# Unread TensorE products behind the last products of each Sobel layer and among the last small products of the layer norm

## The chip, the cores and the metric

The kernel runs on one core of one Trainium2 chip. The metric is the time of one execution on the device in microseconds (us). The kernel before took 2829.04 us, the median of three runs (2828.97 to 2829.38).

## What is computed

The input is an image of 256 x 256 positions with 32 channels in float32. Four layers follow, and each adds its output to its input after a group norm (16 groups). Cut to what matters:

```python
# layer 0: a layer norm over channels, then gated values (the softmax runs over an axis of length 1)
mn = (m - mu) * rsqrt(var + 1e-5) * ln_gamma + ln_beta
x = x + (sigmoid(mn @ Wg) * (mn @ Wv)) @ Wo + bo
# layers 1 and 2: Sobel magnitude of a 3-wide average along one axis
pooled = avg_pool3_same(v)               # v = group_norm(x)
x = x + sqrt(gx(pooled)**2 + gy(pooled)**2 + 1e-6)
# layer 3: two LSTM-like cells with a group norm of the gates, 256 steps in sequence
for t in range(256):
    z = x_t @ W_lat + b_lat
    for j in range(2):
        zz = group_norm([z, h[j]] @ W_cell[j] + b_cell[j])   # 4 groups of 128
        i, f, o, g = split(zz)
        c[j] = sigmoid(f) * c[j] + sigmoid(i) * tanh(g)
        h[j] = sigmoid(o) * tanh(c[j]); z = z + h[j]
    out_t = x_t + z @ W_out + b_out
```

## The kernel before, in words

The image stays in SBUF as `xa` and `xb`: 128 partitions hold four neighbouring columns times 32 channels, and 64 blocks of 256 positions lie along the free axis. Two blocks together, a tile of 128 x 512, are called a pair; there are 32 pairs. The stages run one after the other.

**Input** (to about 42 us). The image is loaded, transposed on TensorE and copied, and statistics for the first group norm are taken.

**Layer norm.** A first loop makes centred values of each pair, squares them on ScalarE and sums the squares with small products into `pvar` (line 247). Then `std`, a `table` load for the sigmoid and `reciprocal` give `rstd` (lines 267 to 269); nine unread products of 128 x 256 run meanwhile (line 271). Then comes the second loop, over the 32 pairs. A product of 32 rows (line 278, `spread` times `rstd`, 128 x 512) spreads the reciprocal deviations over all partitions into a PSUM tile `pb`; VectorE multiplies the pair by it (line 285); ScalarE and GpSimd in turn apply gamma and beta (lines 287 and 291). Four pairs after each other use the four groups of 32 rows in turn. The pool `ps_sp` has eight buffers, one PSUM bank each, so TensorE can be eight products ahead of VectorE. Behind the loop stand four unread products of 128 x 256 (line 296), in one more tile of that name.

**Attention.** The order is written out by hand. Products of 32 rows make values `pv` and gates `pg` (line 313), ScalarE takes the sigmoid (line 328), VectorE multiplies (line 331), and products with 32 output columns project the result (line 337). The pools of PSUM are `ps_g` and `ps_v` with four buffers each, in the banks that `ps_sp` had; the first product waits until those are free.

**Two Sobel layers.** The function `sobel_layer` holds a list of parts with a due time for each of the 32 pairs, sorts it and issues it in that order on every engine. `centre` (lines 447 and 457) and `edges` (line 487) are TensorE products in float32 for two gradients, 1 first and 0 after it; `square` reads them on ScalarE, `total`, `root`, `residual` and `statistics` follow on VectorE and ScalarE. The PSUM tiles `pg1` and `pg0` have three buffers each. Behind a Sobel layer stands a `group_norm` (function at lines 150 to 173): VectorE aggregates the statistics, a product gives the group mean (line 156), VectorE makes `q`, a second product gives the variance (line 165), ScalarE takes the root and VectorE makes scale and bias for the next stage. `busy` (line 143) issues unread products of 128 x 256 around these: three before the first product, two between, and twelve (three before the recurrence) after the second.

**Recurrence.** After the weights are finished with the last scale and bias (lines 689 to 710), 256 steps run, in an order sorted from the due times of `PLAN`. `project` (line 828) and lines 848 and 853 are the gate products, line 910 the transpose of the new state, lines 842, 861 and 902 work of ScalarE, line 866 the sum of squares, line 869 the reciprocal root on GpSimd. Its own `busy` (line 924) issues six unread products of 128 x 256 at the start, and two more a little later.

TensorE writes each float32 product as two records in the profile, of which each streams all columns.

Of the kernel before, what the change touches and what calls it, by code (L numbers as in the profile page):

```python
# [10 lines left out]
F32 = mybir.dt.float32  # L11
# [3 lines left out]
PSUM = bass.MemoryType.PSUM  # L15

S = 256
# [4 lines left out]
P = 128  # L22
# [36 lines left out]
def net_kernel(  # L59
# [20 lines left out]
    nc = tc.nc  # L80
# [13 lines left out]
    ident = cp.tile([P, P], F32, name="ident")  # L94
    make_identity(nc, ident)
    kt = cp.tile([P, NK, P], F32, name="kt")
# [34 lines left out]
    NST = NB // 2  # L131
    one = eps_tile(1.0, "one")

    def table(func, after):

        t = small.tile([P, 1], F32, name="table")
        nc.scalar.activation(t, after, func, scale=0.0, bias=one)
# [56 lines left out]
    with tc.tile_pool(name="nat", bufs=3) as natp, tc.tile_pool(  # L194
        name="ps_in", bufs=4, space=PSUM
# [31 lines left out]
    pairs = [(g * KS + ks, g, ks) for ks in range(KS) for g in range(4)]  # L227

    def pair(t, k):
        return t[:, 2 * k : 2 * k + 2, :].rearrange("p b s -> p (b s)")  # L230

    with tc.tile_pool(name="ln", bufs=4) as lnp:
        rstd = lnp.tile([P, 2 * S], F32, name="rstd", bufs=1)
        with tc.tile_pool(name="ps_ln", bufs=6, space=PSUM) as ps_ln, tc.tile_pool(
            name="ps_var", bufs=1, space=PSUM
        ) as ps_var:
            cen = lnp.tile([P, P], F32, name="cen", bufs=1)
            nc.vector.tensor_scalar(cen, kt[:, K_CEN, :], gn[0], None, ALU.mult)
            pcb = ps_var.tile([P, 1], F32, name="pcb")
            nc.tensor.matmul(pcb, lhsT=kt[:, K_CEN, :], rhs=gn[1], start=True, stop=True)  # L240
            cb = lnp.tile([P, 1], F32, name="cb", bufs=1)
            nc.vector.tensor_copy(cb, pcb)
            pvar = ps_var.tile([P, 2 * S], F32, name="pvar")
            sqs = {}

            def variance(k, g, ks):
                nc.tensor.matmul(
                    pvar[g * C : (g + 1) * C, :],
                    lhsT=avg[:, ks].rearrange("p k j -> p (k j)"),
                    rhs=sqs.pop(k),  # L250
                    start=ks == 0,
                    stop=ks == KS - 1,
                )

            for i, (k, g, ks) in enumerate(pairs):
                pc = ps_ln.tile([P, 2 * S], F32, name="pc")
                nc.tensor.matmul(pc, lhsT=cen, rhs=pair(xa, k), start=True, stop=True)
                sqs[k] = lnp.tile([P, 2 * S], F32, name="sq", bufs=10)
                nc.scalar.activation(sqs[k], pc, AF.Square, bias=cb)
                nc.vector.tensor_scalar(pair(xb, k), pc, cb, None, ALU.add)  # L260
                if g == 3 and ks:
                    for q in pairs[i - 7 : i - 3]:
                        variance(*q)
            for q in pairs[-4:]:
                variance(*q)
            std = lnp.tile([P, 2 * S], F32, name="std", bufs=1)
            nc.scalar.activation(std, pvar, AF.Sqrt, bias=ln_eps)
            table(AF.Sigmoid, std[:, 0:1])
            nc.vector.reciprocal(rstd, std)
            for _ in range(9):  # L270
                nc.tensor.matmul(
                    pvar[:, 0:S], lhsT=ident, rhs=kt[:, 0:2, :], start=True, stop=True
                )
        with tc.tile_pool(name="ps_sp", bufs=8, space=PSUM) as ps_sp:
            for i, (k, g, ks) in enumerate(pairs):
                rows = slice(g * C, (g + 1) * C)
                pb = ps_sp.tile([P, 2 * S], F32, name="pb")
                nc.tensor.matmul(
                    pb,
                    lhsT=spread[rows, ks * J : (ks + 1) * J, :].rearrange("p j c -> p (j c)"),  # L280
                    rhs=rstd[rows, :],
                    start=True,
                    stop=True,
                )
                nc.vector.tensor_mul(pair(xb, k), pair(xb, k), pb)
                if i % 2:
                    nc.scalar.activation(
                        pair(xb, k), pair(xb, k), AF.Identity, scale=gamma4, bias=beta4
                    )
                else:  # L290
                    nc.gpsimd.tensor_scalar(
                        pair(xb, k), pair(xb, k), gamma4, beta4, ALU.mult, ALU.add
                    )
            junk = ps_sp.tile([P, 2 * S], F32, name="pb")
            for _ in range(4):
                nc.tensor.matmul(
                    junk[:, 0:S], lhsT=ident, rhs=kt[:, 0:2, :], start=True, stop=True
                )

# [1 line left out]
    with tc.tile_pool(name="at", bufs=3) as atp, tc.tile_pool(  # L303
        name="ps_g", bufs=4, space=PSUM
# [75 lines left out]
    def sobel_layer(src, dst, scale, bias, between):  # L380
# [5 lines left out]
        ps_s = stack.enter_context(tc.tile_pool(name="ps_s", bufs=3, space=PSUM))  # L386
# [9 lines left out]
        def flat(t):  # L396
            return t.rearrange("p b s -> p (b s)")
# [135 lines left out]
        with tc.manual_schedule():  # L533
            for _, k, part, args in todo:
                part(k, *args)
                if part is statistics and between:
                    between.pop(0)(lambda: flat(ps_s.tile([P, 2, S], F32, name="pg1")))
        stack.close()
        return stats

    stats = sobel_layer(xa, xb, *gn, rw.centring())
    with tc.tile_pool(name="ps_n", bufs=1, space=PSUM) as ps_n:
        gn = group_norm(stats, ps_n, 3, 12)
    stats = sobel_layer(xb, xa, *gn, rw.products())
    second.close()

# [11 lines left out]
    with tc.If(plain > 0) as arms:  # L558
        recurrence(tc, out, ident, weights, inputs, None)
    with arms.Else():  # L560
        recurrence(tc, out, ident, weights, inputs, (gn_gamma, gn_beta))
# [216 lines left out]
def recurrence(tc, out, ident, weights, inputs, general):  # L778

    nc = tc.nc  # L780
# [3 lines left out]
    if general:  # L784
# [7 lines left out]
        with tc.tile_pool(name="ps_w", bufs=2, space=PSUM) as ps_w:  # L792
            for i, dst in enumerate((gam, bet)):
                for l in range(L):
                    pb = ps_w.tile([P, G], F32, name="pb")
                    nc.tensor.matmul(
                        pb, lhsT=ones, rhs=gb[:, i, l * G : (l + 1) * G], start=True, stop=True
# [20 lines left out]
    def at(when, what, *args):  # L818
        todo.append((when, len(todo), what, args))
# [134 lines left out]
        at(((k - inputs.NX + 1) * inputs.XT * J + 2.0) * PERIOD, inputs.load, k)  # L954
    for h in range(2):
        at(-1e5, project, 0, h, 0)
    at(-1e4, busy, 6)
    at(PLAN[1, 1]["x"] - PERIOD, project, 0, 0, 1)
    at(PLAN[1, 1]["x"] - PERIOD, busy, 2)
    for t in range(T):  # L960
# [52 lines left out]
```

## Time and profile before

| What | us |
|---|---|
| median of three runs | 2829.04 |
| the profiled execution | 2832.39 |
| its span, first to last instruction | 2830.5 |
| stretch 0 to 42 (input) | TensorE busy 26.64 of 42.00, clock 0.96 |
| 42 to 77 (layer norm, first loop) | 34.93 of 35.00, clock 1.00 |
| 77 to 104 (root, second loop) | 26.05 of 27.00, clock 0.71 |
| 104 to 323 (attention) | 217.79 of 219.00, clock 0.99 |
| 323 to 478 (first Sobel layer) | 148.95 of 155.00, clock 0.99 |
| 478 to 625 (second Sobel layer) | 141.67 of 147.00, clock 0.99 |
| 625 to 2830 (recurrence) | 2189.04 of 2205.00, clock 1.00 |

The profile is taken of one execution, whose own time is 3.35 us above the median of the runs. Its span begins at the first instruction and ends at the last. The clock is the share of TensorE's full clock that the throttle granted; it is either 0.5 or 1, and a value between the two is a mean over the stretch. A busy TensorE is not a TensorE at its peak: the ends of records are modelled, and records overlap.

### The profile page before, as it was taken

The page shows a single profiled execution, that of the slowest core. Times are in us where ns is not written, and L with a number is a line of the kernel's source. Part 1 is how long each engine was busy: PE and PEld are TensorE (multiplying, and loading weights), DVE is VectorE, ACT ScalarE, POOL GpSimd, SP SyncE. Part 2 cuts the span into 40 slices and gives each one's busy share as a digit, 9 for nine tenths or more (in the row PEclk, how much of TensorE's full clock was granted, in tenths as well). Part 3 has the DMA queues.
Part 4 walks back from the last instruction along what each step waited for, and adds up shares of the span by engine and source line. Part 5 has one row for each costly group of instructions (what it writes and reads, how often), then busy time and mean ns, then how long its engine had stood idle before and what let it go on. Part 6 is the DMA issues. An engine that isn't in the chain of part 4 may idle for free.

```text
span 2830.5 us, 38940 instructions
## 1 busy us (share of the span) xinstructions
PE 2785.1 (98%) x9709; PEld 1051.1 (37%) x9709; DVE 2494.4 (88%) x7272; ACT 2379.3 (84%) x6980; POOL 1299.9 (46%) x1295
## 2 busy tenths in 40 slices
PE   7999999999999999999999999999999999999998
PEld 4433434343333333333333333333333333333332
DVE  6788798978999999999999999999999999999997
ACT  5677676768988888888888888888888888888887
POOL 2211375654444444444444444444444444444443
PEclk9899999999999999999999999999999999999999
DMA  3000000010000000000000000000000000000000
GB/s 136 1 1 1 16 1 1 1 23 6 16 12 12 12 12 12 12 12 12 12 14 12 12 12 12 12 12 12 12 12 12 12 12 14 16 15 12 5 5 8
DMA packets 94337, 38.41 MB, mean 14 GB/s; under 512 B 74852, under 2 KB 91269, under 8 KB 94104
## 3 DMA queue, kind: packets, MB, share of 16 engines
q1 hardware_dynamic: 92612, 34.61, 5.3%
q8 instruction: 82, 1.34, 0.2%
q14 instruction: 151, 1.24, 0.1%
q10 hardware_dynamic: 692, 0.93, 0.1%
q0 software_dynamic: 800, 0.30, 0.0%
HBM read 10.63 MB, written 8.39 MB: 7 GB/s over the span
## 4 chain that ended last, share of the span: by engine, by line
PE 76%; DVE 1%; ACT 0%; issue 0%; POOL 0%; DVEq 0%; POOLq 0%; ACTq 0%
PE zz L853 34%; PE zz L828 19%; PE zz L848 15%; PE pt L910 5%; PE px L933 1%; PE px L930 1%; DVE ve L866 0%; PE px L924 0%; POOL rs L869 0%; ACT sq L861 0%; ACT ga L842 0%; DVE c L890 0%; DVE h L905 0%; DVE fc L894 0%; DVE c L898 0%
## 5 line engine op out<-in xcount | busy, mean ns | idle before, releaser
L869 POOL TENSOR_TENSOR rs<-ve,mhalf 128x4 f32<-128x4 f32 x1024 | 1037.5, 1013 | 1153.5 <-DVE ve L866 1153.5
L853 PE MATMUL zz<-wc,hT 128*128 128x512 f32 x2040 | 1100.3, 621 | 0.5 <-DVE hT L914 0.5
L842 ACT ACTIVATE ga<-zz,rs 128x128 f32<-128x128 f32 x3072 | 927.1, 366 | 32.0 <-POOL rs L869 13.1
L866 DVE TENSOR_REDUCE ve<-sq 128x4 f32<-128x516 f32 x1024 | 707.2, 691 | 123.8 <-ACT sq L861 61.1
L861 ACT ACTIVATE sq<-zz 128x512 f32<-128x512 f32 x1024 | 609.4, 595 | 126.4 <-PE zz L853 116.1
L828 PE MATMUL zz<-fx,xt 33*128 33x512 f32 x2048 | 583.1, 642 | 0.5 <-DVE e L710 0.5
L853 PEld LDWEIGHTS zz<-wc,hT 128*128 128x128 f32 x2040 | 324.0, 188 | 554.3 <-DVE c L898 288.1
L848 PE MATMUL zz<-wc,hT 128*128 128x512 f32 x1024 | 525.0, 594 | 0.0
L902 ACT ACTIVATE th<-c 128x128 f32<-128x128 f32 x1024 | 318.1, 311 | 89.9 <-DVE c L898 80.8
L842 ACT ACTIVATE go<-zz,rs 128x128 f32<-128x128 f32 x1024 | 390.4, 381 | 0.0
L890 DVE TENSOR_TENSOR c<-ga 128x128 f32<-128x128 f32 x1024 | 295.8, 289 | 39.2 <-ACT ga L842 25.2
L910 PEld LDWEIGHTS pt<-ident,h 128*128 128x128 f32 x1024 | 142.8, 139 | 502.1 <-DVE h L905 501.5
L914 DVE COPY hT<-pt 128x128 f32<-128x128 f32 x1024 | 292.6, 286 | 26.0 <-PE pt L910 4.0
L910 PE MATMUL pt<-ident,h 128*128 128x128 f32 x1024 | 299.5, 292 | 8.1 <-DVE h L905 8.1
L905 DVE TENSOR_TENSOR h<-go,th 128x128 f32<-128x128 f32 x1024 | 291.9, 285 | 11.8 <-ACT th L902 1.5
L894 DVE TENSOR_TENSOR fc<-ga,c 128x128 f32<-128x128 f32 x1020 | 297.5, 292 | 0.6 <-ACT ga L842 0.6
L898 DVE TENSOR_TENSOR c<-c,fc 128x128 f32<-128x128 f32 x1020 | 288.1, 282 | 6.8
L828 PEld LDWEIGHTS zz<-fx,xt 33*128 33x128 f32 x2048 | 156.3, 185 | 258.9 <-ACT go L842 193.7
L331 DVE TENSOR_TENSOR o<-pv,sg 128x512 f32<-128x512 f32 x256 | 158.1, 681 | 43.6 <-PE pg L313 37.7
L848 PEld LDWEIGHTS zz<-wc,hT 128*128 128x128 f32 x1024 | 162.3, 198 | 70.8 <-issue 40.8
L328 ACT ACTIVATE sg<-pg 128x512 f32<-128x512 f32 x256 | 138.6, 599 | 31.4 <-PE pg L313 26.7
L313 PE MATMUL pv<-xb,wv 32*128 32x512 f32 x512 | 156.5, 620 | 0.0
(154 smaller groups left out, 2174.5 us busy)
## 6 DMA issues: line engine op xcount, KB each, us to landing
xt<-xa SPq DMA_DIRECT2D x256, 64.0 KB, 2.0
nat<-in_x_dram SPq DMA_DIRECT2D x16, 512.0 KB, 7.9
out_dram<-st SPq DMA_DIRECT2D x254, 32.0 KB, 1.6
wc<-in_L_conv_W_cell_dram SPq DMA_DIRECT2D x2, 512.0 KB, 4.4
kt<-in_consts_dram ACTq DMA_DIRECT2D x1, 832.0 KB, 5.8
wv<-in_L_conv_Wv_dram POOLq DMA_DIRECT2D x4, 32.0 KB, 5.1
wg<-in_L_conv_Wg_dram POOLq DMA_DIRECT2D x4, 32.0 KB, 6.7
gamma<-in_L_conv_ln_gamma_dram POOLq DMA_DIRECT2D x4, 0.1 KB, 5.9
```

The source lines that it names most:

```text
L828: nc.tensor.matmul(zz, lhsT=x, rhs=fx[rows, l, :], start=True, stop=l == 0 and t == 0)
L842: nc.scalar.activation(dst, gates(x, g), func, scale=scale)
L848: nc.tensor.matmul(get("zz"), lhsT=v["hT", 0, t][:, seqs], rhs=wc[:, l, 0, :], start=False, stop=t == 0)
L853: nc.tensor.matmul(get("zz"), lhsT=v["hT", l, t - 1][:, seqs], rhs=wc[:, l, 1, :], start=False, stop=True,)
L861: nc.scalar.activation(sqs[l, h][:, :, 0:H], four(get("zz")), AF.Square, scale=float(H**-0.5))
L866: nc.vector.tensor_reduce(ve, sqs[l, h], AX.X, ALU.add)
L869: nc.gpsimd.tensor_tensor(rs, get("ve"), inputs.mhalf, ALU.pow)
L890: nc.vector.tensor_mul(c, gates(get("ga"), 0), gates(get("ga"), 3))
L894: nc.vector.tensor_mul(fc, gates(get("ga"), 1), get("c"))
L902: nc.scalar.activation(th, get("c"), AF.Tanh)
L910: nc.tensor.transpose(pt[:, 0:P], get("h"), ident)
L914: nc.vector.tensor_copy(v["hT", l, t][:, seqs], get("pt")[:, 0:P])
```

## The change

Three places are edited. In the layer norm's second loop, the pool has seven buffers for `pb` and one bank for an unread tile `junk`; behind each of the last ten small products stands one unread product of 128 x 128, and the four unread products behind the loop are gone. In each Sobel layer, right behind the last `edges`, nine unread products of 128 x 256 are issued into a buffer of `pg1`. At the start of the recurrence, eight unread products stand where six stood. The order of instructions on VectorE, ScalarE, GpSimd and SyncE stays the same.

```diff
-        with tc.tile_pool(name="ps_sp", bufs=8, space=PSUM) as ps_sp:
+        with tc.tile_pool(name="ps_sp", bufs=7, space=PSUM) as ps_sp:
+            junk = ps_sp.tile([P, 2 * S], F32, name="junk", bufs=1)
             for i, (k, g, ks) in enumerate(pairs):
...
-            junk = ps_sp.tile([P, 2 * S], F32, name="pb")
-            for _ in range(4):
-                nc.tensor.matmul(
-                    junk[:, 0:S], lhsT=ident, rhs=kt[:, 0:2, :], start=True, stop=True
-                )
+                if i >= len(pairs) - 10:
+                    nc.tensor.matmul(
+                        junk[:, 0:P], lhsT=ident, rhs=kt[:, 0, :], start=True, stop=True
+                    )
...
             for _, k, part, args in todo:
                 part(k, *args)
+                if part is edges and args == (0,) and k == NST - 1:
+                    junk = flat(ps_s.tile([P, 2, S], F32, name="pg1"))
+                    for _ in range(9):
+                        nc.tensor.matmul(
+                            junk[:, 0:S], lhsT=ident, rhs=kt[:, 0:2, :], start=True, stop=True
+                        )
...
-    at(-1e4, busy, 6)
+    at(-1e4, busy, 8)
```

## The prediction

> **What bounds the kernel now.** I read the page's first two parts first. The PE is busy 98% of the span, but the recurrence takes 2205 of the 2830.5 us and the change touches none of its steady state. So I went to the places edited, and there the busy share says little: what counts is which wait ends last, and at which clock the PE runs.
>
> ```profile
> PE 2785.1 (98%) x9709; PEld 1051.1 (37%) x9709; DVE 2494.4 (88%) x7272; ACT 2379.3 (84%) x6980; POOL 1299.9 (46%) x1295
> PEclk9899999999999999999999999999999999999999
> ```
>
> Next I cut the layer norm's end into stretches at the moments where the granted clock changes. They lie 3.413 us apart (columns: length, busy us and count of PE, weight loads, DVE, ACT, POOL; then clock).
>
> ```profile
> 84.79:88.20 3.41, 3.41 (x14) 1.58 (x12) 3.41 (x7) 2.26 (x4) 2.23 (x4) 1.00 0.01 2
> 88.20:91.61 3.41, 3.41 (x12) 2.76 (x12) 3.41 (x7) 2.30 (x3) 2.14 (x4) 0.50 0.00 0
> 91.61:95.03 3.42, 3.42 (x15) 2.86 (x12) 3.42 (x7) 2.44 (x3) 2.15 (x4) 0.50 0.02 5
> 95.03:98.44 3.41, 3.41 (x14) 2.60 (x11) 3.41 (x7) 2.44 (x3) 2.14 (x4) 0.50 0.00 0
> 98.44:101.85 3.41, 3.41 (x9) 1.85 (x6) 3.41 (x7) 2.27 (x3) 2.17 (x3) 0.50 0.00 0
> 101.85:105.27 3.42, 3.31 (x12) 1.22 (x10) 0.52 (x1) 0.99 (x2) 0.77 (x1) 0.50 0.00 0
> ```
>
> DVE is full to 102.4 while the PE, which only feeds it, runs at half clock. The reader should see that PE "busy" is 100% there too and yet the clock stays down: busy records are not what the clock follows. The small products use 32 of 128 rows.
>
> The group and the timeline give the two rates and the hand-over:
>
> ```profile
> L285 DVE TENSOR_TENSOR xb<-xb,pb 128x512 f32<-128x512 f32 x31 | 18.6, 680 | 0.0
> ```
>
> ```profile
> 97.64 2.07 PE L278 MATMUL pb<-rstd,spread 32*128 32x512 f32 x3
> 98.66 1.05 PE L278 MATMUL pb<-rstd,spread 32*128 32x512 f32 x1
> 99.64 0.79 PE L296 MATMUL pb<-kt,ident 128*128 128x256 f32 x1
> 100.23 1.06 PE L296 MATMUL pb<-kt,ident 128*128 128x256 f32 x2
> ...
> 99.64 3.78 PE L296 MATMUL pb<-kt,ident 128*128 128x256 f32 x8
> 103.53 1.98 PE L313 MATMUL pg<-xb,wg 32*128 32x512 f32 x8
> ```
>
> DVE takes one product per 18.6/31 = 0.60 us. Every product is two records. Last, the gap between the Sobel layers:
>
> ```profile
> 472.99 2.01 PE L143 MATMUL junk<-kt,ident 128*128 128x256 f32 x6 [3.02 <-DVE xb L504]
> 474.79 0.48 PE L156 MATMUL pm<-mv,kt 128*128 128x1 f32 x2
> 475.13 2.05 PE L143 MATMUL junk<-kt,ident 128*128 128x256 f32 x4
> 476.98 0.42 PE L165 MATMUL pv<-q,kt 128*128 128x1 f32 x2
> ```
>
> The PE is idle for 3.02 us, the clock is 0.50 from 473.91 to 477.32, and the two filler products (four records) in front of the variance product then take 2.05 us, though its operand is ready by 475.9 (DVE's mean, difference and q at 475.3 to 475.9).
>
> [...]the first four small products start at 82.0 within 0.02 us of each other, and every passage between 33-row and 128-row products in the recurrence leaves a gap.[...] I counted each record by the time that its columns stream, times its share of the array's rows and columns: the stretch from 84.79 has 3.41/0.60 = 5.7 products of 0.85 us on a quarter of the rows, so it is filled 5.7 x 0.85/4/3.41 = 0.35; at half clock the same stream fills 0.71. So counted, 0.35 and less lost the clock (84.79, 313.48, 470.49), 0.44 kept it (467.08), 0.71 at half clock did not bring it back (91.61, 95.03), and 0.77 and more did (473.91).
>
> **The layer norm, step by step.** Rates at half clock: a 256-column record every (3.78 - 0.59 - 0.63)/6 = 0.43 us, so 0.85 for 512 columns and 0.21 for 128. One small product holds its row group from 97.64 to 98.66 + 0.85 = 99.51, that is 1.87 us (0.16 of it the exposed weight load). Before, four row groups overlap, so the PE needs 1.71/4 = 0.43 per product, less than DVE's 0.60. The change puts a 128-row product behind each of the last ten. It needs all four row groups, so product n+1 can no longer run beside product n[...]. The switch from 32 to 128 rows is in the lines above: the last stream ends 99.51, the next load starts 99.64,[...] then 0.16 of load (100.23 - 99.64 - 0.43). At full clock the recurrence shows the same in both directions, near 0.2. One pair at half clock: 1.87 + 0.13 + 0.16 + 0.43 + 0.13 = 2.71 us, against DVE's 0.60. Filled share of a pair: (1.71/4 + 0.43)/2.71 = 0.32, far under what brings the clock back, so it stays at half throughout. 2.71 is my value; at full clock the same pair would be 0.85 + 0.21 + 0.4 = 1.47.
>
> Start: with seven buffers instead of eight, product 22 waits for multiply 15; the multiplies end at 102.37 and are 0.60 apart, so that is 92.8 (before: 92.26). The smaller pool alone costs nothing, since DVE still has six multiplies in hand. Product 22 ends at 94.73, its filler at 95.45, product 23 streams from 95.74, product 31 from 95.74 + 8 x 2.71 = 117.4 to 119.15, the last filler ends 119.87. DVE's last multiply ends near 120.0. The first attention product waits for that multiply, for the PE's own filler, and starts near 120.15 instead of 103.53: **+16.6 us**. Removed are four products at the end (3.78 us, 1.1 us of them after DVE's last multiply); that saving is inside the difference. ACT and POOL follow DVE and have room.
>
> Then attention begins cold. Before, the clock rises 1.7 us after its start, because the four removed fillers filled that window. Now the window holds a product on one row group, a filler and four products: about 0.65 to 0.7, too little. The next holds the stall on ACT's first sigmoid (0.72 in the trace) at half rate. I expect the rise in the third window, some 9 us after the start. By then DVE's first product is 2.2 us later behind the start than before (7.0 against 108.30 - 103.53 = 4.8: two sigmoid-paced products at double length). A block of attention at half clock needs 24 products x 1.71/4 + 0.6 for switches = 10.9 us, against 123.37 - 116.69 = 6.7 in the trace, so the last 2 us lose 0.8: 3.0 in all; with the rise a window earlier 1.7, at once 0.3. I take **+2.3**.
>
> **The Sobel ends.** Nine 128x256 products follow the last edges, 9 x 0.43 = 3.9 us at full clock: 469.95 + 0.2 to about 474.0, behind DVE's 472.84 for the next pool. They cover the idle time, so the clock should not fall. The three fillers then run 474.1 to 475.4, the mean product is read at 475.6 instead of 475.3, q is ready at 476.2, the two fillers take 0.9 instead of 2.05, and the variance reaches ACT at 476.65 instead of 477.44: **-0.8**. At the second end, same sum from 616.9: fillers to 621.0 and 622.3, ACT's square root at 623.65 instead of 624.30: **-0.65**. Bounds: were the clock already half at the edges, nine products would take 7.7 us and each end would be about 3 us later; nothing in the trace says so (0.44 filled, clock 1.00). Queued behind the nine is only the group norm; they wait for an old buffer of pg1 which DVE released at 466.5. ACT's squares wait for the edges, not for them. Instruction order on DVE, ACT, POOL and SP is unchanged.
>
> **Eight instead of six at the recurrence's start.** In the trace these run at half clock from 631.95 to 637.4, and the first transpose, whose h is ready at 636.4, waits for them. Two more cost 2 x 0.85 = 1.7 at half clock, or nothing at full clock (six end before 635). The stretch before (627.5 to 630.9, 0.31 filled) will lose the clock again, but where the grid lies against it is open. I take **+0.4** (0 to 1.7). The end of attention, where the clock also drops (316.9), may fall otherwise on the grid: 0, +-1.
>
> **Sum.** 16.6 + 2.3 - 0.8 - 0.65 + 0.4 = **+17.85 us**. Against the profiled execution (2832.39, span 2830.5) that is 2850.2; that execution lies 3.35 above the median of the runs, and I carry the difference to the median: 2829.04 + 17.85 = **2846.9 us**.
>
> **Rivals.** (a) *No serialisation, not slower*: if the fillers could run beside the small products, a pair costs the PE 0.43 + 0.43 = 0.85, ten end at 101.4, attention starts at DVE's 102.45 (-1.1) and warm (-0.6): 2829.04 - 1.7 - 1.45 + 0.4 = **2826.3**. The deciding price is the pair: up to 1.06 us (ten pairs between 92.8 and 103.4) the end of this stage does not move. For it: small products do run in parallel among themselves. Against it: a 128-row product needs the rows that they hold[...]. (b) *The clock comes up inside the ten pairs*, say at 98.44 after two: the others at 1.47 bring the last multiply to 110.5, +7.1 - 0.6 - 1.05: **2834.5**. Against it: 0.71 filled did not suffice in three windows in a row. (c) *The grid falls badly at the later ends* (half clock at an edge or for all eight): +3 to +5 on my sum, **2851**.
>
> **How the numbers follow.** My case 0.77, (a) 0.09, (b) 0.08, (c) 0.06. The likeliest one's own range, from pairs of 2.5 to 2.9 us and 0.3 to 3.5 at attention's start, is 2843 to 2851. A measurement here can tell about 0.2%, 5.7 us, from no change. Faster by more: 0.01, the low end of (a); within: the rest of (a) and half of (b), 0.12; slower: 0.87. The range runs from 2838, inside the upper part of (b), to 2851.5.
>
> **What would show it.** In the profile after: a pitch near 2.7 us for the last ten small products, DVE waiting for pb from about 95 on, attention's first product near 120, half clock from 88.2 to beyond 122; no clock drop right after either Sobel layer and the square root 0.6 to 0.8 earlier against the layer's last edges. A pitch of 0.6 to 0.9 would make the prediction wrong, and so would a clock of 1.00 between 95 and 118.

## The result and the profile after

| | us |
|---|---|
| before, median of 4 runs beside the changed kernel | 2829.21 |
| after, median of 4 runs (2849.64 to 2851.32) | 2850.27 |
| ratio of after to before, 95% interval | 1.0073 (1.0055 to 1.0090) |
| predicted | 2846.9 (2838.0 to 2851.5) |

The changed kernel is slower by 21 us of the medians, where 17.85 were forecast. The profiled execution took 2850.13, its span is 2848.3. On the page, TensorE gains busy share and its clock row loses a tenth at the start; neither says what happened.

```profile
PE 2810.1 (99%) x9761; PEld 1062.1 (37%) x9761; DVE 2496.1 (88%) x7272; ACT 2379.2 (84%) x6980; POOL 1300.7 (46%) x1295
PEclk9799999999999999999999999999999999999999
```

In the two profiles, any two changes of the granted clock lie a whole number of 3.413 us apart (88.20 and 105.27 before: five; 86.96 and 127.92 after: twelve). A window, here as in the recorded texts, is one stretch of that grid. The windows around the pairs, as shown for before (length, busy us of PE, weight loads, DVE, ACT, POOL, then the clock), tell what happened:

```profile
83.55:86.96 3.41, 3.41 (x14) 1.70 (x12) 3.41 (x7) 2.44 (x3) 2.14 (x4) 1.00 0.00 0
86.96:90.37 3.41, 3.41 (x13) 2.61 (x12) 3.41 (x7) 2.30 (x3) 2.14 (x4) 0.50 0.00 0
...
93.79:97.20 3.41, 3.41 (x5) 1.34 (x6) 1.94 (x4) 1.85 (x3) 1.54 (x2) 0.50 0.00 0
...
110.85:114.27 3.42, 3.42 (x6) 1.00 (x4) 0.69 (x1) 0.81 (x1) 0.09 (x1) 0.50 0.00 0
...
124.51:127.92 3.41, 3.41 (x20) 2.57 (x15) 2.48 (x4) 2.17 (x4) 0.00 (x0) 0.50 0.00 0
127.92:131.33 3.41, 3.41 (x27) 1.99 (x23) 2.96 (x5) 2.48 (x5) 0.00 (x0) 1.00 0.00 0
```

VectorE (DVE), full before to the end of this stage, works only 0.69 of 3.42 us in the stretch from 110.85, while TensorE (PE) is "busy" throughout with less than half of the records. The clock stays at half for 41 us (86.96 to 127.92) instead of 17 (88.20 to 105.27). The fillers that should lift it sink the filled share: 0.29 to 0.34 in the windows with pairs, by the prediction's count, against 0.71 before. The timeline has the pairs, and VectorE's waits, before and after, show what took over:

```profile
112.00 0.80 PE L296 MATMUL junk<-kt,ident 128*128 128x128 f32 x2
112.72 2.07 PE L279 MATMUL pb<-rstd,spread 32*128 32x512 f32 x2
114.72 0.80 PE L296 MATMUL junk<-kt,ident 128*128 128x128 f32 x2
115.45 2.07 PE L279 MATMUL pb<-rstd,spread 32*128 32x512 f32 x2
117.45 0.80 PE L296 MATMUL junk<-kt,ident 128*128 128x128 f32 x2
118.50 2.09 PE L313 MATMUL pg<-xb,wg 32*128 32x512 f32 x8 [0.26 <-PE junk L296]
```

```profile
DVE xb L285 <- PE pb L278: 2.0, 1, 2.0
DVE xb L286 <- PE pb L279: 19.0, 10, 2.0
```

The first line is of before, the second of after (us in total, times, longest). A small product comes every 115.45 - 112.72 = 2.73 us, and VectorE is idle for 19.0 us in front of its multiplies. Before, its only such wait was the 2.0 us for the first product; these 2.0 are in the 19.0 too, so the pairs add 17.0.

At the first Sobel layer's end the nine fillers close the gap, the clock stays at 1.00, and the two products of the group norm follow with fillers at full speed between:

```profile
485.95 4.15 PE L539 MATMUL pg<-kt,ident 128*128 128x256 f32 x18
490.16 1.56 PE L143 MATMUL junk<-kt,ident 128*128 128x256 f32 x6
491.56 0.28 PE L156 MATMUL pm<-mv,kt 128*128 128x1 f32 x2
491.78 1.13 PE L143 MATMUL junk<-kt,ident 128*128 128x256 f32 x4
492.75 0.28 PE L165 MATMUL pv<-q,kt 128*128 128x1 f32 x2
```

By stage, from the same instructions in the two profiles (us, starts of records; "root" is ScalarE's line 168):

| from - to (each row begins where the one above ends) | before | after | difference | predicted |
|---|---|---|---|---|
| start - first small product | 81.99 | 80.04 | -1.95 | 0 |
| - attention's first product | 21.54 | 38.46 | +16.92 | +16.6 |
| - 32nd multiply of attention | 27.71 | 30.42 | +2.71 | +2.3 |
| - last multiply of attention | 187.19 | 187.20 | 0.01 | 0 |
| - root of the next group norm | 10.19 | 8.54 | -1.65 | 0, +-1 |
| - last edges of Sobel layer 1 | 140.76 | 140.77 | 0.01 | 0 |
| - root | 8.06 | 7.63 | -0.43 | -0.8 |
| - last edges of Sobel layer 2 | 138.80 | 138.82 | 0.02 | 0 |
| - root | 8.06 | 7.63 | -0.43 | -0.65 |
| - fifth state copy (hT) of the recurrence | 28.85 | 30.78 | +1.93 | +0.4 |
| - end | 2177.36 | 2178.05 | +0.69 | 0 |

### The profile page after: what moved, and what is told of

Its sections match the earlier page's. It is cut to its first block, busy times and chain, and to the rows that moved or that the text cites. A ratio compares the mean times of both kernels' runs of the same rounds, so it can differ in the third digit from the quotient of the medians.

```text
span 2848.3 us, 39046 instructions
## 1 busy us (share of the span) xinstructions
PE 2810.1 (99%) x9761; PEld 1062.1 (37%) x9761; DVE 2496.1 (88%) x7272; ACT 2379.2 (84%) x6980; POOL 1300.7 (46%) x1295
## 4 chain that ended last, share of the span: by engine, by line
PE 76%; DVE 1%; ACT 0%; issue 0%; POOL 0%; DVEq 0%; POOLq 0%; ACTq 0%
PE zz L859 34%; PE zz L834 19%; PE zz L854 15%; PE pt L916 5%; PE px L939 1%; PE px L936 1%; DVE ve L872 0%; PE px L930 0%; POOL rs L875 0%; ACT sq L867 0%; ACT ga L848 0%; DVE c L896 0%; DVE h L911 0%; DVE fc L900 0%; DVE c L904 0%
```

## The experiments

My theory: a 128-row filler between 32-row products takes away their running side by side and adds two changes between 32 and 128 rows, with a gap at each (0.13 us before, 99.51 to 99.64), so each of the ten pairs takes 2.73 us against VectorE's 0.60; the rest is attention's cold start. The main rival: the fillers cost by their own work, or the loss sits in the other two places. Each kernel was timed in several runs beside the kernel before, whose runs in one series of 49 spread from 2826.09 to 2834.66 with a median of 2830.07. So an effect of 1 or 2 us is read from the stages of a profile, and one of 5 from the times.

### The layer norm's edit alone

```diff
-        with tc.tile_pool(name="ps_sp", bufs=8, space=PSUM) as ps_sp:
+        with tc.tile_pool(name="ps_sp", bufs=7, space=PSUM) as ps_sp:
+            junk = ps_sp.tile([P, 2 * S], F32, name="junk", bufs=1)
...
+                if i >= len(pairs) - 10:
+                    nc.tensor.matmul(
+                        junk[:, 0:P], lhsT=ident, rhs=kt[:, 0, :], start=True, stop=True
+                    )
```

(and the four behind the loop gone)

> Of the change only the layer norm's edit: seven buffers, ten 128x128 fillers between the last ten small products, none behind. Theory 1 (a 128-row filler between 32-row products ends their running side by side, at half clock a pair takes 2.73 us, and attention then starts cold): nearly the whole loss is here, +19 to +20 us, 2848 to 2850, small products 2.73 apart, clock up some 9 us after attention starts. Rival (the loss sits at the Sobel ends or at the recurrence's start): under +10 us.

Measured: 2849.48, ratio 1.0075 (1.0061 to 1.0089). From the first small product to attention's first product 38.46 us, the same as in the whole change. The loss is here; the other two edits together leave nothing that the times can tell. The clock rises 8.1 us after attention's first product (9.4 in the whole change), and the 32nd multiply of attention comes 29.78 us after that product (30.42 there, 27.71 before).

### The Sobel fillers alone

```diff
+                if part is edges and args == (0,) and k == NST - 1:
+                    junk = flat(ps_s.tile([P, 2, S], F32, name="pg1"))
+                    for _ in range(9):
+                        nc.tensor.matmul(
+                            junk[:, 0:S], lhsT=ident, rhs=kt[:, 0:2, :], start=True, stop=True
+                        )
```

> Of the change only the nine fillers behind each Sobel layer's last edges. Theory 1 (they keep the clock, the two group norms' roots come 0.4 us earlier each, but the drop of the clock at the recurrence's start may only move): -1 to +1 us, 2828 to 2830, no clock drop at either end of a Sobel layer. Rival (they add to the loss): +1.5 us or more.

Measured: 2828.71, ratio 0.9999 (0.9991 to 1.0008). In the profile each root is 0.43 us earlier against the last edges, and the clock drops at neither end. But from the last root to the fifth state copy it takes 30.76 us instead of 28.85 (28.43 to 29.87 in the nine profiles without these fillers): the clock now falls at 627.15, 4.1 us after the root, and stays down for 10.2 us, in the middle of the products that finish the weights. In this profile the gain of 0.86 is more than given back there. Its execution took 2832.47, 3.8 us above the median of its own kernel, and the times show neither a gain nor a loss.

### Eight instead of six at the recurrence's start, alone

```diff
-    at(-1e4, busy, 6)
+    at(-1e4, busy, 8)
```

> Of the change only eight fillers instead of six at the recurrence's start. If they run at half clock there, they hold up the first transpose by up to 1.7 us: 0 to +1.7 us, 2829 to 2831. Rival (they shorten the time at half clock): -1 us.

Measured: 2832.09, ratio 1.0008 (1.0001 to 1.0014). In the profile the last root lies 29.87 us ahead of the fifth copy (28.85 before), but the same stretch took 29.72 in the profile of the next kernel, which has six. At the fifth copy the two more fillers seem free, but at the first transpose they are not. In these two profiles the clock first falls behind the root at nearly the same place (6.9 and 7.0 us after it), and the new state is ready 13.02 us after the root in both; the transpose, which stands behind the fillers, starts 14.84 us after the root with eight and 14.01 with six. By the fifth copy 0.15 us of this is left, since with six the clock is at half for another 3.4 us, from 647.85, and with eight it is not. The times speak for a small loss, and its size stays open.

### The ten fillers together behind the loop

```diff
-                if i >= len(pairs) - 10:
+            for _ in range(10):
```

(against the layer norm's edit; the filler itself as there)

> The layer norm's edit alone, but with the same ten 128x128 fillers put together behind the last small product. Theory 1 (only the place between the small products costs): ten fillers at half clock take 4.27 us instead of 3.78 for the four that they replace, attention starts 0.5 to 0.7 later, +0.7 us, 2829.9; small products stay 0.60 apart. Rival (the fillers' own work or the seventh buffer costs): more than +10 us, as with the fillers between.

Measured: 2830.68, ratio 1.0005 (0.9998 to 1.0012); attention's first product 22.99 us after the first small one (21.54 before), 1.45 later where I had expected 0.5 to 0.7. VectorE waits only for the first small product, 2.0 us, as before. Neither seven buffers instead of eight nor the work of ten fillers is what costs.

### Fillers on the same 32 rows

```diff
+                if i >= len(pairs) - 10:
+                    nc.tensor.matmul(
+                        pb[:, 0:P], lhsT=ident[rows, :], rhs=kt[rows, 0, :], start=True, stop=True
+                    )
```

(ahead of each of the last ten small products, seven buffers, none behind)

> The layer norm's edit alone, but each of the ten fillers is a 128x128 product of 32 rows, on the same row group as its small product and ahead of it, into the same pb tile, which the small product then overwrites; no filler behind.[...] Theory 1: a pair holds one row group 1.87 + 0.43 us, four run side by side, 0.58 a pair, so VectorE's 0.60 still sets the pace; attention starts 1 us earlier but cold, clock up two or three windows later: 0 to +2.5 us. Rival (any further product in this loop costs about 2 us): more than +10 us.

Measured: 2831.17, ratio 1.0007 (0.9998 to 1.0015). VectorE waits only for the first product, as before:

```profile
DVE xb L289 <- PE pb L282: 2.0, 1, 2.0
```

Attention's first product comes 20.49 us after the first small one, 1.05 earlier than before. Ten more products among the same ten, as long as the fillers before, hold nothing up here, where each keeps to the 32 rows of its own small product. They even bring the clock up, at 93.73. But nothing fills the time behind them (TensorE idles 2.89 us ahead of attention's first product, at 100.27), the clock falls again at 100.56, just after attention's start, and the 32nd multiply comes 29.31 us after that start instead of 27.71. That the loss in this stage is gone doesn't say which counts more in the whole change, the gaps between 32 and 128 rows or the rows that a filler takes from the other small products: these fillers do neither.

### All ten in one block

```diff
-                if i >= len(pairs) - 10:
-                    nc.tensor.matmul(
-                        junk[:, 0:P], lhsT=ident, rhs=kt[:, 0, :], start=True, stop=True
-                    )
+                if i == len(pairs) - 10:
+                    for _ in range(10):
+                        nc.tensor.matmul(
+                            junk[:, 0:P], lhsT=ident, rhs=kt[:, 0, :], start=True, stop=True
+                        )
```

> The layer norm's edit alone, but all ten 128x128 fillers stand in one block behind product 23 of 32; then nine small products follow without fillers. Same number of products,[...] and the small products run side by side again. Theory 1: the block takes 4.3 us at half clock, less what VectorE has in hand; the last multiply is some 4.5 us later; attention starts cold (+2 to +3): +4 to +7 us. Rival (each filler costs 2 us wherever it stands before the last product): +17 us or more.

Measured: 2834.84, ratio 1.0016 (1.0008 to 1.0024), +4.8 of the medians.

```profile
94.98 4.09 PE L297 MATMUL junk<-kt,ident 128*128 128x128 f32 x20
99.01 3.62 PE L279 MATMUL pb<-rstd,spread 32*128 32x512 f32 x18
```

The same twenty filler records take 4.09 us in one block, and the nine small products behind them 3.62 us, side by side. In the whole change the ten fillers and the nine products between them took 25.3 us (92.91 to 118.25). The block also brings the clock up, at 98.36, so its nine products run at full clock; at half clock before, VectorE got one every 0.60 us, which would be 5.4 for nine. In the profile attention's first product comes 2.1 us later than before (23.63 us after the first small product), and the rest of the loss is a cold start: the clock has fallen again at 105.19, and the 32nd multiply comes 30.55 us after attention's first product instead of 27.71.

### Five pairs instead of ten

```diff
-                if i >= len(pairs) - 10:
+                if i >= len(pairs) - 5:
```

> The layer norm's edit alone with a filler behind each of the last five small products instead of the last ten. Theory 1: five pairs less at 2.73 - 0.60 = 2.13 us: 10.7 us less than the layer norm's edit alone; attention's first product 28 us after the first small product (38.5 with ten, 21.5 before), start still cold: +8 to +9.5 us in all. Rival (a cost at the start of the interleaving, such as the seventh buffer or the cold clock alone): +15 us or more.

Measured: 2837.78, ratio 1.0026 (1.0016 to 1.0037); attention's first product 27.81 us after the first small one. Five pairs less save 38.46 - 27.81 = 10.65 us, 2.13 a pair, which is 2.73 - 0.60. From five to ten the loss grows with the pairs. The first five cost less, 27.81 - 21.54 = 6.27 us together instead of 10.65; the prediction's own terms, six multiplies in hand at 0.60 and 1.1 us of removed fillers, make up about the difference. Attention's cold start comes on top with five pairs as with ten (2.1 us to the 32nd multiply). A price at the entry, of seven buffers or of the half clock alone, does not show.

### Fillers of one column

```diff
-                        junk[:, 0:P], lhsT=ident, rhs=kt[:, 0, :], start=True, stop=True
+                        junk[:, 0:1], lhsT=ident, rhs=kt[:, 0, 0:1], start=True, stop=True
```

> The layer norm's edit alone, but each of the ten fillers streams 1 column instead of 128. Theory 1: the filler's own 0.43 us is the smallest part of a pair; what costs is that the small product stands alone (1.87)[...]: about 2.3 us a pair instead of 2.73, attention's first product 34 us after the first small product (38.5 with 128 columns), +14 to +17 us in all. Rival (the filler's streaming is what costs): a pair falls to VectorE's 0.60, within 3 us of before.

Measured: 2845.99, ratio 1.0062 (1.0048 to 1.0076).

```profile
110.10 0.59 PE L296 MATMUL junk<-kt,ident 128*128 128x1 f32 x2
110.61 2.07 PE L279 MATMUL pb<-rstd,spread 32*128 32x512 f32 x2
112.61 0.59 PE L296 MATMUL junk<-kt,ident 128*128 128x1 f32 x2
113.13 2.07 PE L279 MATMUL pb<-rstd,spread 32*128 32x512 f32 x2
```

A pair still takes 113.13 - 110.61 = 2.52 us, with next to nothing streamed; I had expected 2.3. Of the 2.13 that a pair loses, the 127 columns are 0.21. The filler's two records and the next small product still start 0.23 and 0.28 us apart; what takes that time was not followed.

### The four old fillers behind as well

```diff
+            for _ in range(4):
+                nc.tensor.matmul(
+                    junk[:, 0:S], lhsT=ident, rhs=kt[:, 0:2, :], start=True, stop=True
+                )
```

(against the layer norm's edit)

> The layer norm's edit with its ten fillers between, and the four 128x256 fillers of before behind them as well. Theory 1: the four hold attention up by 2.7 to 3.4 us more, but bring the clock up within a window or so, so that its cold start (2.7 us) is mostly gone: -1 to +2 us against the edit alone, clock up 0 to 4 us after attention's first product instead of 9. Rival (the four are pure cost): +3.4 us against the edit alone, clock up as late as there.

Measured: 2848.26, ratio 1.0069 (1.0055 to 1.0083). Attention starts 3.26 us later than with the edit alone (41.72 against 38.46), but the clock is up at that moment:

```profile
118.92:122.33 3.41, 3.31 (x9) 2.08 (x9) 0.00 (x0) 0.73 (x1) 0.00 (x0) 0.50 0.00 0
122.33:125.74 3.41, 2.71 (x18) 1.32 (x20) 0.00 (x0) 2.23 (x5) 0.00 (x0) 1.00 0.00 0
```

and the 32nd multiply of attention is only 0.34 us later than there. So the cold start is worth some 2.9 us here. The four fillers of before had bought off all but some 0.9 of it: to the 32nd multiply, attention took 27.71 us before and 26.86 here.

### A version meant to be faster, with three fillers, then four

```diff
+                if part is edges and args == (0,) and k == NST - 1:
+                    junk = flat(ps_s.tile([P, 2, S], F32, name="pg1"))
+                    for _ in range(9):
+                        nc.tensor.matmul(
+                            junk[:, 0:S], lhsT=ident, rhs=kt[:, 0:2, :], start=True, stop=True
+                        )
...
-            for _ in range(4):
+            for _ in range(3):
...
-        gn = group_norm(stats, ps_n, 3, 3)
+        gn = group_norm(stats, ps_n, 3, 6)
```

> The kernel before with the nine fillers behind each Sobel layer, three instead of four fillers behind the layer norm's small products, and six instead of three behind the last group norm's variance. Theory 1: attention starts 0.9 us earlier, the two roots 0.4 us each, and the drop of the clock comes later at the recurrence's start: -2 to -3 us, about 2827. Rival (the clock is lost again behind the new fillers, or attention starts cold): within 1 us of before.

Measured: 2827.56 against 2830.04 beside it, ratio 0.9991 (0.9982 to 0.9999). The last root to the fifth copy takes 27.66 us (28.85 before, 30.76 with the Sobel fillers alone): the clock now falls 7.3 us after the root, behind the products that finish the weights, and for 3.4 us only. But my step for three fillers failed. Attention starts 0.86 us earlier and cold, the clock comes up at 111.19, and the 32nd multiply is 1.98 us later than before, counted from the first small product.

With the fourth filler put back:

> The kernel with Sobel fillers and six fillers in the last group norm, but with the layer norm's four fillers of before kept (it had three, and attention began cold). Theory 1: attention starts 1.1 us later than with three but warm, which saves some 2 us: -0.5 to -2 us against that kernel, 2826 to 2827. Rival (the window's place decides, not the fourth filler): within 0.5 us of that kernel.

Measured: 2827.10 against 2828.31 beside it, ratio 0.9994 (0.9986 to 1.0003). In the profile attention starts warm and its 32nd multiply is 2.17 us earlier than with three fillers. The times of the two versions can't be told apart, and that either beats the kernel before by more than 2 us is not shown.

## Why the prediction was right

**The pairs.** Forecast 2.71 us (the terms as written add up to 2.72), measured 2.73, in place and in cause. Fillers of one column instead of 128 leave 2.52 a pair; fillers on the same rows leave no wait of VectorE; one block leaves 4.8 us of 19; each pair less saves 2.13. The step from the two gaps of the trace of before to the price of a pair held. Both gaps that the prediction put at 0.13 are there: the last stream of a small product ends at 113.74 + 0.85 = 114.59, and the filler's weights are loaded from 114.72; the filler's last stream ends at 115.10 + 0.21 = 115.31, and the next small product's weights are loaded from 115.45. By the prediction's arithmetic the larger part of the 2.13 is another, 1.87 - 0.60 = 1.27: before, small products ran side by side (VectorE took one every 0.60 us, while the last held its rows for 1.87, from 97.64 to 99.51), and now each stands alone, with the fillers' loads at 112.00 and 114.72 around the one from 112.72. No run tells these two parts from each other, and none has the pairs at full clock; 1.47 us for a pair there stays an estimate from the gaps in the recurrence of before (at 1002.25 + 0.43 = 1002.68 the last stream on 33 rows ends, the load for 128 rows starts at 1002.77 and leaves 0.11 exposed, 0.2 together).

**The clock.** The filled share, counted with rows and columns, was 0.29 to 0.34 in the stretches with pairs, and the clock stayed down to 127.92, 9.4 us after attention's first product; I had put it at 9. Attention's start cost 2.71, forecast 2.3: the case that came was priced at 3.0, and I had left half a chance to an earlier rise. The size goes with the moment of the rise: in the seven profiles in which the clock rises 7.1 to 9.7 us after attention's start this stretch is 1.6 to 2.8 us longer than before, and the later the rise, the longer.

**The Sobel ends.** Right in kind, half in size: 0.43 each for 0.8 and 0.65. At the first end I had the root 7.27 us after the last edges; it comes after 7.63. The nine fillers cost what I had put for them: the three behind them start 490.16 - 485.43 = 4.73 us after the last edges' record, forecast 4.72. What I sized too small are the terms behind them. The mean is read 6.44 us after the last edges, not 6.22, since the three fillers take 1.40 us where I had 1.3, and 0.31 us pass from the mean product's start to its reading where I had 0.2. The variance then loses another 0.14. Why these steps take longer than the streams in them was not tried.

**The recurrence's start.** Forecast +0.4, measured +1.93 to the fifth copy. I priced the two fillers of line 930 and put nothing for what the Sobel fillers may do here. Before, the clock is down ahead of the root, which comes at 624.30, and again 6.6 us after it:

```profile
617.27:620.68 3.41, 0.83 (x4) 0.78 (x5) 2.28 (x4) 0.96 (x2) 3.36 (x2) 1.00 0.43 98
620.68:624.09 3.41, 3.41 (x12) 2.65 (x10) 1.35 (x4) 0.00 (x0) 3.30 (x3) 0.50 0.37 80
624.09:627.51 3.42, 2.55 (x10) 1.52 (x10) 1.89 (x6) 1.84 (x3) 3.31 (x3) 1.00 0.44 101
627.51:630.92 3.41, 2.90 (x10) 1.35 (x9) 1.01 (x3) 0.73 (x2) 0.81 (x1) 1.00 0.47 105
630.92:634.33 3.41, 3.41 (x8) 1.92 (x7) 0.69 (x1) 1.33 (x5) 1.05 (x1) 0.50 0.37 85
634.33:637.75 3.42, 3.42 (x10) 2.31 (x9) 1.24 (x4) 1.34 (x6) 1.01 (x1) 0.50 0.01 2
```

After, the root comes at 639.51, and the clock falls 3.8 us after it, in the midst of the products that finish the weights:

```profile
639.92:643.33 3.41, 2.18 (x8) 1.14 (x8) 2.19 (x6) 1.45 (x2) 3.30 (x3) 1.00 0.43 97
643.33:646.75 3.42, 2.97 (x7) 1.42 (x6) 1.11 (x3) 0.59 (x1) 0.63 (x1) 0.50 0.45 102
646.75:650.16 3.41, 3.41 (x5) 0.91 (x4) 0.69 (x1) 0.60 (x1) 0.19 (x1) 0.50 0.24 54
650.16:653.57 3.41, 3.41 (x9) 2.69 (x10) 0.72 (x2) 1.83 (x6) 0.86 (x1) 0.50 0.00 0
```

From the root to the fifth copy the clock is at half for 10.2 us in both (before, the last 3.4 of them from 647.99), so it is the place that counts, not the length. The first state copy splits the loss: it comes 13.38 us after the root before (13.5 to 14.3 in the seven other profiles with six fillers and no Sobel fillers), 15.20 with the Sobel fillers alone, and 16.06 after. So up to 1.82 go with the Sobel fillers and 0.86 with the two more fillers, behind which the transpose waits. At the fifth copy the Sobel fillers alone show the same 30.76 as the whole change, but only because that kernel is at half clock once more, from 647.63, and the changed one is not.

Two things limit this reading. First, 0.41 of the 1.82 is not the clock: VectorE's last instruction on `sb` ends 10.26 us after the last edges with the Sobel fillers and 10.28 before, each time less than 0.1 us behind the end of one of GpSimd's memsets (line 747 after, 741 before), so the second root's gain does not reach the weights. That the memset holds it was not tried. Second, it is open whether the Sobel fillers bring the drop forward. A boundary of the 3.413 us grid lies 3.8 to 4.1 us after the root in all four profiles with them, and 2.1 to 3.6 in the nine without, and no run moves the one without the other.

The +0.69 us from the fifth copy to the end is not traced; the same stretch, with the same code, took 2176.5 to 2178.1 us in the thirteen profiles.

**The sum.** The two profiled spans lie 17.83 us apart, 17.85 were forecast; that they agree so well is partly luck, since -1.95 and -1.65 are not the change's (below) and stand against terms that I had put too low. Without these two the stages give +21.4, near the 21 of the medians: about 0.3 too low in the pairs, 0.4 at attention's start, 0.6 at the Sobel ends, 1.5 and 0.7 in the recurrence.

## What to carry to other kernels

By these runs, a filler that is to keep TensorE's clock up should not stand among products that run side by side on 32 rows each: a filler of 128 rows made each of them stand alone (2.73 us a pair instead of 0.60), and the filled share fell instead of rising (0.29 to 0.34, from 0.71). Fillers on the same rows held nothing up, and neither did fillers in one block where TensorE would wait (VectorE's wait for the small products stayed at 2.0 us in both). But they should reach up to the next work: where they did not, the clock fell again 0.3 us after attention's first product (100.56, same rows) and 0.5 us before it (105.19, one block ahead of nine products). And follow the clock past the place that is mended, and other engines too: what is gained at one place may be lost a few microseconds later, to a drop at a worse place (0.86 us of the Sobel ends against 1.91 from the last root to the fifth copy, with the Sobel fillers alone) or to an instruction that ends no earlier than before.

## What was not expected of the hardware

At the end of attention, whether the clock drops goes with how the 3.413 us grid of its changes lies in an execution. Five of the thirteen profiles, before among them, have a drop there and need 10.2 us from its last multiply to the next root; the others need 8.54 or 8.55. In the five, a boundary of the grid lies 1.1 to 1.7 us ahead of that multiply, in the others 0.6 to 0.7 or at least 1.9.

The input stage varies too, but not for this reason. The four profiles with a drop near 23 us (before among them) reach the first centring product (line 257) at 39.4 to 40.3, the others at 37.8 to 39.0. This goes with the input's transfers: from 14 us to the drop at 23.35, TensorE's transposes waited 3.4 us for them before, and in the same stretch 0.5 after. In all thirteen profiles the product starts 8.0 to 8.9 us after the last landing of the input on record. So the drop comes behind the waits, and why the transfers took longer is open.

So a single profile of before is 3 us off its own median for no fault of the code, and two profiles are best compared stage by stage.
